# Far sums of a graph recurrence: four batches or eight in one matmul

## The chip, the cores and the metric

The kernel runs on one core of one Trainium2 chip. A time is the device time of one execution in microseconds. Before the change the median of three runs is 4688.69 us (4688.29 to 4690.42).

A core has engines with one instruction queue each, worked through in order: TensorE (matmuls, in the profile PE, with the weight loads as PEld), VectorE (DVE), ScalarE (ACT), GpSimd (POOL), and SyncE (SP), which only issues DMAs here. They wait for each other by semaphores. TensorE writes to PSUM[...].

## The reference, cut to what matters

Sixteen graphs (batches) of 1024 nodes with 256 features pass through four layers, each of the form x = x + layer(relu(layernorm(x)), adj). The change is in layer 2, a recurrence over the nodes:

```python
def step(h, i):
    x = jnp.take(h_e, i, axis=1)
    row = jnp.take(norm_adjT, i, axis=1)
    x_par = jnp.einsum('bj,bjd->bd', row, h)
    iou = x @ W_ioux.T + b_ioux + x_par @ W_iouh.T + b_iouh
    r, z = jnp.split(iou, 2, axis=1)
    r, z = (jax.nn.sigmoid(r), jax.nn.sigmoid(z))
    hc = jnp.tanh(x @ W_coux.T + b_coux + x_par * r @ W_couh.T + b_couh)
    h_new = z * x_par + (1.0 - z) * hc
    h = jax.lax.dynamic_update_slice(h, h_new[:, None, :], (0, i, 0))
    return (h, None)
h_out, _ = jax.lax.scan(step, h_e, jnp.arange(n))
```

Node i needs x_par, the weighted sum over all nodes j: the new h for j < i, the old one for j >= i. The matrix is sparse (some 3% of the entries), so nodes that do not depend on each other can be computed together.

## The kernel before, in words

Layers 0 and 1 run first, batch by batch, then the recurrence (layer 2), then layer 3. All arithmetic is in float32.

**The recurrence.** The 1024 nodes are cut into 8 blocks of 128 (index t in the code), and a block into 8 sub-blocks of S = 16 (index s, 0 to 7). A table made earlier orders the nodes within a block so that nodes in a sub-block mostly do not depend on each other. One step (t, s) computes the 16 nodes of a sub-block for all 16 batches, 256 columns in all: `x` is the sum over parents, `round_` (lines 817 to 849) makes the gates and the new state, first the r, z and c matmuls (line 788, tiles pr, pz, pc), then sigmoid and tanh on ScalarE (lines 829, 834, 835, 845) and the products on VectorE (lines 830, 839, 846, 847), ending in `hT`. `turned` (lines 851 to 860) transposes hT on TensorE (line 856) and copies it to `h` or `dh` on ScalarE (line 859). Sub-blocks 5 and 6 take a second round (line 995 on) for the dependencies inside a sub-block, with an exchange by `x_change` (line 813, copies `dx` in lines 988 and 989) between the rounds, and sub-block 7 takes four. A branch (line 1006) runs further rounds where a chain of dependencies is longer.

**What later sub-blocks get from a finished one.** With h of sub-block s in hand, its contributions are added: to the next sub-block at once (`near`, line 1029), to the next block's first sub-block in `next_block` (line 757), and to all that lie further ahead in the block in `far_tasks` (lines 761 to 780). The columns that the far sum of sub-block s covers are far = 128 - (s + 2) * 16 per batch: 96, 80, 64, 48, 32, 16 for s = 0 to 5, and none after. The batches come in two groups (G2 = 2) of eight (GB = 8). A far sum is one matmul of a 128-column slice of h with a masked, spread out adjacency `bd` (line 716, on GpSimd) into a PSUM tile `pf`, and one addition by VectorE of that tile to `bxt` (line 773), where the sums over parents are gathered.

**Fillers.** TensorE would wait for the other engines during a step. So each step has a list of tasks, `todo` (lines 919 to 938), mixed from two lists: `behind`, the far sums of the sub-block before, and `share`, the base products of the next block (`base_tasks`: seven matmuls of 256 columns at line 623 for each batch, a scaled copy `bs` to SBUF at line 610 with a 0/1 matrix `to` at line 607, and two transposes, the "turn", at line 637 with a copy at line 638). The far sums of sub-blocks 2 to 5 are therefore worked off in steps 3 to 6. A list is emptied in proportion, and steps of one round take base products while between 6 and 9 tasks are on the list (line 935).

`fill(weight)` (lines 942 to 948) pops tasks at a few places of the step until their summed costs, which each task carries as a number, reach that place's share. A task puts its matmuls into the program there, and its bank-emptying part on the list `late`, which `evict()` puts into VectorE's and ScalarE's program at the end of that stretch, behind the step's own arithmetic:

```python
late.append(task() or (lambda: None))
```

The order of TensorE, VectorE, ScalarE and GpSimd is that of the program text (line 884), so a change of a task's cost or length changes where all tasks stand.

**Banks.** Far sums, base products, turns and the gate matmuls (line 735) share the tile name pf with three buffers of one bank each. A matmul that needs a bank waits until the instruction that reads the earlier tile in it is done. A base product holds its bank over its seven matmuls and until its copy bs.

**DMA.** `load` (lines 588 to 597) fetches the adjacency `ab` and the states `hb` of a base product one batch ahead through SyncE's queue, and line 601 masks one 128x128 part on GpSimd. GpSimd also issues the gathers `aj` (line 700) and the scatters of h (line 1022).

Of the kernel before, what the change touches and what calls it, by code (L numbers as in the profile page):

```python
# [9 lines left out]
F32 = mybir.dt.float32  # L10
# [6 lines left out]
P = 128  # L17
B, N, D, H = 16, 1024, 256, 1024
NT = N // P
DC = D // P  # L20
HC = H // P
S = 16
NS = P // S
G2 = 2
GB = B // G2
# [15 lines left out]
def gnn_stack(ctx: ExitStack, tc: tile.TileContext, a: dict, out: bass.AP):  # L41
    nc = tc.nc
# [505 lines left out]
    def layer_2(shared, early):  # L548
        with ExitStack() as st:
            wp = st.enter_context(tc.tile_pool(name="w2", bufs=1))  # L550
            psum = st.enter_context(tc.tile_pool(name="psum2", bufs=1, space=PSUM))
# [201 lines left out]
            def next_block(h, bd, n, start):  # L753

                for c in range(DC):
                    for g in range(G2):
                        nc.tensor.matmul(pnx[:, c, g * GR : (g + 1) * GR], h[:, g, c * P : (c + 1) * P],
                                         bd[:, g, :, n : n + S], start=start and c == 0 and g == 0, stop=True,
                                         skip_group_check=True)

            def far_tasks(bxt, h, sub):


                bd, s = sub.bd, sub.s
                far = P - (s + 2) * S

                def task(g, c, b4):
                    def run():
                        pf = psum.tile([P, 4, far], F32, name="pf", bufs=3)
                        nc.tensor.matmul(pf, h[:, g, c * P : (c + 1) * P], bd[:, g, b4 : b4 + 4, S : S + far],  # L770
                                         start=True, stop=True)
                        to = bxt[:, c, g * GB + b4 : g * GB + b4 + 4, P - far :]
                        return lambda: nc.vector.tensor_add(to, to, pf)  # L773
                    return 0.0067 * far, run
                tasks = []
                if far > 0:
                    tasks = [task(g, c, b4) for g in range(G2) for c in range(DC) for b4 in (0, 4)]
                if sub.n > P - s * S:
                    tasks.insert(0, (0.9, lambda: next_block(h, bd, P - (s + 1) * S, s == 0)))
                return tasks  # L780
# [103 lines left out]
            with tc.manual_schedule(engines={mybir.EngineType.PE, mybir.EngineType.DVE, mybir.EngineType.Activation, mybir.EngineType.Pool}):  # L884
# [3 lines left out]
                bxt = shared.tile([P, DC, B, P], F32, name="bxt")  # L888
# [14 lines left out]
                for t in range(NT):  # L903
# [10 lines left out]
                    for s in range(NS):  # L914
# [38 lines left out]
                        for c in range(DC):  # L953
                            to = x[:, c].rearrange("p (b i) -> p b i", b=B)
# [13 lines left out]
                        h = work.tile([P, G2, D], F32, name="h")  # L968
# [56 lines left out]
                        if s + 1 < NS:  # L1025
                            near = psum.tile([P, DC, G2 * GR], F32, name="pa")
                            for c in range(DC):
                                for g in range(G2):
                                    nc.tensor.matmul(near[:, c, g * GR : (g + 1) * GR], h[:, g, c * P : (c + 1) * P],
                                                     sub.bd[:, g, :, :S], start=True, stop=True)  # L1030
                            behind = far_tasks(bxt, h, sub)
                        elif t + 1 < NT:
                            next_block(h, sub.bd, 0, False)
                            near = pnx
                            behind = last_tasks(t + 1, bxt_next)
                            bxt, he = bxt_next, he_next
# [302 lines left out]
    with tc.tile_pool(name="shared", bufs=2) as shared:  # L1339
        x, hn, at, h = {}, {}, {}, {}  # L1340
# [49 lines left out]
```

## Time and profile before

| what | value |
|---|---|
| median of three runs | 4688.69 us |
| profiled execution, its time | 4692.98 us |
| its span | 4691.1 us |
| granted TensorE clock, mean | 0.976 |
| recurrence, page time | 1522.6 to 3404.1 us |
| step 3 of block 1 | 1837.9 to 1862.9 us |
| step 4 of block 2 | 2105.7 to 2130.1 us |
| steps 5 and 6 of block 1 | 1895.2 to 1924.1, 1924.1 to 1952.8 us |
| matmuls of far sums (line 770) | 768 records, 214.5 us busy |
| additions of far sums (line 773) | 384, 141.5 us busy |
| base products (line 623) | 1568 records, 420.8 us busy |

A step is counted from one sum of x (line 956) to the next. In rows of the profile, an operation is given as output <- inputs, with partitions x columns; "xN" is a count; the bracket in a timeline row is the time that the engine stood idle ahead of it, and what ended that. A float32 matmul leaves two MATMUL records, and with them two weight loads. The recorded end of a matmul is modelled; how long one occupies TensorE is read from one start to the next.

The additions take, by columns (mean of 64 each): 0.552 us for 384, 0.486 for 320, 0.419 for 256, 0.352 for 192, 0.284 for 128 and 0.217 for 64.

### The profile page before, as it was taken

The page shows a single profiled execution, that of the slowest core. Times are in us where ns is not written, and L with a number is a line of the kernel's source. Part 1 is how long each engine was busy: PE and PEld are TensorE (multiplying, and loading weights), DVE is VectorE, ACT ScalarE, POOL GpSimd, SP SyncE. Part 2 cuts the span into 40 slices and gives each one's busy share as a digit, 9 for nine tenths or more (in the row PEclk, how much of TensorE's full clock was granted, in tenths as well). Part 3 has the DMA queues.
Part 4 walks back from the last instruction along what each step waited for, and adds up shares of the span by engine and source line. Part 5 has one row for each costly group of instructions (what it writes and reads, how often), then busy time and mean ns, then how long its engine had stood idle before and what let it go on. Part 6 is the DMA issues. An engine that isn't in the chain of part 4 may idle for free. (4 is left out here: it accounts for less than half of the span.)

```text
span 4691.1 us, 55474 instructions
## 1 busy us (share of the span) xinstructions
PE 4365.5 (93%) x19479; PEld 2999.7 (64%) x19479; DVE 2551.8 (54%) x6564; ACT 1280.5 (27%) x2741; POOL 1622.2 (35%) x1914
## 2 busy tenths in 40 slices
PE   8899799999897999999999999999899999999998
PEld 4444345555454777777778777777655656565666
DVE  6667945446544444444444444445456666666665
ACT  1111112221211232323232322222323333333332
POOL 3223234333432323232222233333245353535352
PEclk9999899999998999999999999999899999999999
DMA  4333234565545544444434444442042323232310
GB/s 148 120 110 96 87 92 162 180 204 163 163 136 186 158 127 148 130 153 137 149 110 155 132 144 146 158 132 84 31 157 81 108 81 108 81 108 81 108 45 19
DMA packets 530992, 576.81 MB, mean 123 GB/s; under 512 B 42544, under 2 KB 439472, under 8 KB 528304
## 3 DMA queue, kind: packets, MB, share of 16 engines
q1 hardware_dynamic: 499536, 460.27, 31.5%
q0 software_dynamic: 31040, 111.44, 6.7%
q8 instruction: 207, 3.39, 0.3%
q14 instruction: 209, 1.71, 0.1%
HBM read 469.65 MB, written 116.65 MB: 125 GB/s over the span
## 5 line engine op out<-in xcount | busy, mean ns | idle before, releaser
L295 PE MATMUL pa<-at,h 128*128 128x512 f32 x1088 | 495.3, 608 | 32.8 <-DVE ag L300 32.8
L623 PE MATMUL pf<-hb,ab 128*128 128x256 f32 x1568 | 420.8, 387 | 29.0 <-DVE bxt L773 16.3
L295 PE MATMUL pa<-at,q 128*128 128x512 f32 x960 | 424.7, 595 | 0.0
L295 PEld LDWEIGHTS pa<-at,h 128*128 128x128 f32 x1088 | 209.6, 195 | 277.3 <-issue 231.4
L735 PE MATMUL pf<-hs,wx 128*128 128x256 f32 x1536 | 348.8, 381 | 20.2 <-POOL hs L726 18.1
L735 PEld LDWEIGHTS pf<-hs,wx 128*128 128x128 f32 x1536 | 290.4, 191 | 62.8 <-POOL hs L726 19.9
L623 PEld LDWEIGHTS pf<-hb,ab 128*128 128x128 f32 x1568 | 278.7, 193 | 69.3 <-DVE bxt L773 23.5
L295 PEld LDWEIGHTS pa<-at,q 128*128 128x128 f32 x960 | 178.5, 190 | 216.6 <-issue 212.8
L1188 PE MATMUL ph<-bxt,hb 128*128 128x512 f32 x704 | 309.3, 595 | 3.9 <-ACT hb L1172 3.1
L1217 POOL TENSOR_TENSOR ss<-ss,sq 128x512 f32<-128x512 f32 x224 | 280.5, 1271 | 87.9 <-ACT sq L1215 84.1
L770 PE MATMUL pf<-bd,h 128*128 128x384 f32 (+5 forms) x768 | 214.5, 373 | 48.4 <-DVE bxt L773 26.5
L1022 POOL DMA_INDIRECT hs_d<-h,table x128 | 129.2, 1010 | 371.2 <-ACT gates L743 185.6
L1278 PEld LDWEIGHTS po<-w,hh 128*128 128x128 f32 x2048 | 236.2, 193 | 9.5 <-issue 7.2
L1278 PE MATMUL po<-w,hh 128*128 128x128 f32 x2048 | 240.3, 277 | 1.4 <-ACT hh L1261 0.7
L1188 PEld LDWEIGHTS ph<-bxt,hb 128*128 128x128 f32 x704 | 132.6, 191 | 163.9 <-issue 159.0
L773 DVE TENSOR_TENSOR bxt<-bxt,pf 128x384 f32<-128x384 f32 (+5 forms) x384 | 141.5, 385 | 146.8 <-PE pf L770 144.3
L740 DVE TENSOR_TENSOR gates<-pf,bias 128x512 f32<-128x512 f32 x128 | 88.3, 691 | 220.5 <-PE pf L735 220.5
L1260 DVE TENSOR_TENSOR hh<-hh,po 128x512 f32<-128x512 f32 x256 | 154.5, 681 | 96.7 <-PE po L1257 96.7
L83 POOL TENSOR_TENSOR rs<-rs_v,mhalf 128x8 f32<-128x8 f32 (+1 forms) x65 | 106.8, 1643 | 252.8 <-DVE rs_v L79 239.4
L770 PEld LDWEIGHTS pf<-bd,h 128*128 128x128 f32 x768 | 132.5, 192 | 93.2 <-DVE bxt L773 41.9
L1215 ACT ACTIVATE sq<-hh 128x512 f32<-128x512 f32 x224 | 141.2, 630 | 164.3 <-DVE hh L1213 126.2
L829 ACT ACTIVATE r<-pr 128x256 f32<-128x256 f32 (+3 forms) x230 | 68.0, 347 | 415.2 <-PE pr L788 400.9
(296 smaller groups left out, 8548.4 us busy)
## 6 DMA issues: line engine op xcount, KB each, us to landing
at<-in_adjT SPq DMA_DIRECT2D x64, 1024.0 KB, 7.0
ab<-in_adj SPq DMA_DIRECT2D x128, 512.0 KB, 3.8
bxt<-in_adjT SPq DMA_DIRECT2D x88, 512.0 KB, 6.4
at<-in_adjT SPq DMA_DIRECT2D x40, 512.0 KB, 6.6
ad<-in_adj SPq DMA_DIRECT2D x128, 128.0 KB, 6.7
x_d<-x POOLq DMA_DIRECT2D x16, 1024.0 KB, 5.4
he_d<-h POOLq DMA_DIRECT2D x16, 1024.0 KB, 8.9
heT_d<-hT POOLq DMA_DIRECT2D x16, 1024.0 KB, 4.4
```

Source lines behind the costliest of these rows:

```text
L83: nc.gpsimd.tensor_tensor(r, t, mhalf.to_broadcast(shape), ALU.pow)
L295: nc.tensor.matmul(pa, h[:, mt, c * P : (c + 1) * P], at[n0 // 512][:, mt], start=mt == 0, stop=mt == NT - 1)
L623: nc.tensor.matmul(pb, ab[:, jts[k]], hb[:, jts[k]], start=k == 0, stop=k == len(jts) - 1)
L735: nc.tensor.matmul(pg[:, e], wx[:, c, q * D + e * P : q * D + (e + 1) * P], self.hs[:, c], start=c == 0, stop=c == DC - 1)
L770: nc.tensor.matmul(pf, h[:, g, c * P : (c + 1) * P], bd[:, g, b4 : b4 + 4, S : S + far], start=True, stop=True)
L773: return lambda: nc.vector.tensor_add(to, to, pf)
L1022: nc.gpsimd.indirect_dma_start(out=hs_d[t][g][:, :], out_offset=row(1, g, t, s), in_=h[:, g], in_offset=None)
L1188: nc.tensor.matmul(pa, h[b][:, mt, c * P : (c + 1) * P], at[b][n0 // NH][:, mt], start=mt == 0, stop=mt == NT - 1)
L1215: nc.scalar.activation(sq, hh[q][:, k], AF.Square)
L1217: nc.gpsimd.tensor_tensor(ss[q], ss[q], sq, ALU.add)
L1260: nc.vector.tensor_mul(hh[q][:, k], hh[q][:, k], pr)
L1278: nc.tensor.matmul(po[:, n], left[:, c, n * P : (n + 1) * P], right[:, c], start=onto is None and n == 0 and c == 0, stop=c == HH - 1, ski ...
```

## The change

Where eight batches fit into one bank (far * 8 <= 512, so for sub-blocks 2 to 5), a far sum takes all eight batches of a group: matmuls of 512, 384, 256 and 128 columns take the place of two each of 256, 192, 128 and 64, and one addition that of two. Sub-blocks 0 and 1 (768 and 640 columns for eight) stay as they are. The cost that a task carries changes with it, from 0.0067 * far for four batches to 0.0017 * far for each batch (0.0136 * far for eight).

```diff
                 far = P - (s + 2) * S
-
-                def task(g, c, b4):
+                n = 4 if far * GB > 512 else GB
+
+                def task(g, c, b0):
                     def run():
-                        pf = psum.tile([P, 4, far], F32, name="pf", bufs=3)
-                        nc.tensor.matmul(pf, h[:, g, c * P : (c + 1) * P], bd[:, g, b4 : b4 + 4, S : S + far],
+                        pf = psum.tile([P, n, far], F32, name="pf", bufs=3)
+                        nc.tensor.matmul(pf, h[:, g, c * P : (c + 1) * P], bd[:, g, b0 : b0 + n, S : S + far],
                                          start=True, stop=True)
-                        to = bxt[:, c, g * GB + b4 : g * GB + b4 + 4, P - far :]
+                        to = bxt[:, c, g * GB + b0 : g * GB + b0 + n, P - far :]
                         return lambda: nc.vector.tensor_add(to, to, pf)
-                    return 0.0067 * far, run
+                    return 0.0017 * n * far, run
                 tasks = []
                 if far > 0:
-                    tasks = [task(g, c, b4) for g in range(G2) for c in range(DC) for b4 in (0, 4)]
+                    tasks = [task(g, c, b0) for g in range(G2) for c in range(DC) for b0 in range(0, GB, n)]
```

One line more stands in the function, so lines from 767 on carry a number higher by one in the changed kernel.

## The prediction

> **What bounds the kernel now.** I read the shares of busy time first, then the costliest groups, the waits of TensorE inside the recurrence, and the timeline of single steps. "Step s" is sub-block s (0 to 7) of a block; the far sums of sub-blocks 2 to 5 run as fillers in steps 3 to 6, so these steps change. In the page, TensorE has 93% of the span, and the two groups that the change touches are these.
>
> ```profile
> PE 4365.5 (93%) x19479; PEld 2999.7 (64%) x19479; DVE 2551.8 (54%) x6564; ACT 1280.5 (27%) x2741; POOL 1622.2 (35%) x1914
> ...
> L770 PE MATMUL pf<-bd,h 128*128 128x384 f32 (+5 forms) x768 | 214.5, 373 | 48.4 <-DVE bxt L773 26.5
> ...
> L773 DVE TENSOR_TENSOR bxt<-bxt,pf 128x384 f32<-128x384 f32 (+5 forms) x384 | 141.5, 385 | 146.8 <-PE pf L770 144.3
> ```
>
> A float32 matmul leaves two records, so 768 are 384 far sums, 64 of each of six widths. TensorE idles ahead of them for the adds that empty their banks. The waits of the weight loads (PEld), which run ahead of the matmuls, within the recurrence (page time 1547 to 3430 us; in total, times, longest):
>
> ```profile
> PEld pf L770 <- DVE bxt L773: 41.9, 39, 2.0
> PEld pf L623 <- DVE bxt L773: 23.5, 18, 1.4
> PEld pf L770 <- ACT bs L610: 21.3, 21, 1.1
> PEld pf L770 <- DVE bxt L638: 14.7, 14, 1.1
> ```
>
> All four are one thing, a wait for one of the three "pf" banks: 101.4 us together. Is it on the path? In the timeline of block 1, step 3 (start, duration):
>
> ```profile
> 1846.58 1.03 PE L623 MATMUL pf<-hb,ab 128*128 128x256 f32 x4
> 1847.44 1.03 PE L770 MATMUL pf<-bd,h 128*128 128x256 f32 x4
> ...
> 1848.54 0.49 ACT L610 ACTIVATE bs<-pf,dinv 128x256 f32<-128x256 f32 x1
> 1849.08 0.70 PE L770 MATMUL pf<-bd,h 128*128 128x256 f32 x2 [0.61 <-ACT bs L610]
> ...
> 1849.68 0.42 DVE L847 TENSOR_TENSOR hT<-z,w 128x256 f32<-128x256 f32 x1
> ...
> 1850.22 1.08 DVE L773 TENSOR_TENSOR bxt<-bxt,pf 128x256 f32<-128x256 f32 x3
> 1850.69 0.70 PE L623 MATMUL pf<-hb,ab 128*128 128x256 f32 x2 [0.91 <-DVE bxt L773]
> ...
> 1853.73 0.60 PE L856 MATMUL pa<-ident,hT 128*128 128x128 f32 x4
> ```
>
> hT is done at 1850.10, but the transposes that need it (L856) start at 1853.73: they are queued on TensorE behind fillers, and the fillers stand still twice for a bank, whose add sits on VectorE behind the very chain that makes hT. So bank waits lengthen the step one for one. Step 5 has the larger case:
>
> ```profile
> 1903.85 0.42 DVE L847 TENSOR_TENSOR hT<-z,w 128x256 f32<-128x256 f32 x1
> 1904.20 0.28 DVE L773 TENSOR_TENSOR bxt<-bxt,pf 128x128 f32<-128x128 f32 x1
> ...
> 1904.53 0.49 PE L770 MATMUL pf<-bd,h 128*128 128x128 f32 x2 [1.57 <-DVE bxt L773]
> ...
> 1905.94 0.60 PE L856 MATMUL pa<-ident,hT 128*128 128x128 f32 x4
> ```
>
> **What the skill says.** "VectorE: DVE Perf Modes", section on the TRN2 errata, gives a float32 tensor_tensor (N+151)/0.96 ns: 691 at 512 columns, 424 at 256. The trace has 692 (L740) and 419, so one add of 512 for two of 256 saves 0.146 us; it agrees. "PSUM — Partial Sum Buffer", the four PSUM rules: one matmul output is at most one bank, 512 fp32; eight batches of 64 columns are just that. "Perfetto Trace Analysis", Identifying Performance Opportunities: a gap that repeats on the engine that should be saturated can mean too few buffers; that is what the four rows show. "TensorE: Matmul & The Clock Gate", Part 1: after an idle window of about 3.4 us TensorE runs at half rate; in block 7, steps 5 and 6, this trace has 128-column passes 0.21 us apart where elsewhere they are 0.11.
>
> **The change, part by part.** 128 matmuls and 128 adds go (4 steps x 8 blocks x 4). From starts in the timelines one far sum takes 0.43 us on TensorE at 256 columns, 0.86 at 512, 0.33 at 192, 0.65 at 384, 0.22 at 128, and 0.17 to 0.22 at 64. Pairs are free of gain except the narrowest: 4 x 8 x about 0.17 = 5 us. VectorE loses 128 x 0.14 = 18 us of work, which lies beside TensorE's and is worth nothing by itself. The gain is in banks: a merged sum holds one where two held two. The built order of TensorE, in steps of blocks 0 to 6, between the last candidate matmul ("pc") and the transposes T:
>
> Before, steps 3 and 4: 2 base, 3 far, base, far, base, turn, far, 2 base, T. After: 3 base, far, 2 base, far, turn, 2 base, T. Before, step 5: far, turn, base, far, 2 base, far, T; after: turn, base, far, 2 base, T.
>
> *Step 3* (base product 0.43, turn 0.22). Before: 4.95 us of work in 7.15, so 2.2 of stall. After: base end 1847.88, far 1848.74, 2 base 1849.60. The second far takes the bank of the finished base product; its "bs" copies come 0.43 later than before, since that product ends 0.43 later (free at 1849.46): no wait, end 1850.46. The turn needs the first far's bank. Its add follows hT, which is itself 0.43 late because the tanh stands behind the "bs" copy on ScalarE: start 1850.65, 0.69 long, so turn at 1851.39, T at 1852.47. Gain 1.26.
>
> *Step 4* (block 2, from its start): pc ends 8.47 (a smaller first filling, 0.11), base 9.77, far 10.42, 2 base 11.28, second far from 11.41 ("bs" ends 11.36) to 12.06, first add 12.54 to 13.10, turn 13.15, T 14.23 against 15.38. Gain 1.15.
>
> *Step 5* (block 1, from its start). pc ends 6.74. Turn, base, far and 2 base need three banks and wait for none: they end at 8.68 and T waits for hT instead. Block 7 shows that state: in its step 5 T ends 2.69 after pc, and the exchange (L813) starts 0.96 later, behind the copies of "dh". So T ends 9.43, base and far fit in, L813 at 10.39 (before 12.15). Then 0.87 of exchange and 1.73 of fillers: the second round begins at about 13.03 (14.43). It keeps its 3.47, so pc ends at 16.50; turn, 2 base, far, base 1.94: T at 18.44 (20.76). After it two base instead of two base and a far: 0.22. Gain 2.54.
>
> *Step 6*, likewise: L813 at 10.39 (12.00), round 12.80 (14.20), pc end 16.23, T ends 18.40 (21.02), 0.22 after. Gain 2.84.
>
> Per block 7.79, times seven 54.5. Block 7 has no base products: in step 3 T ends at 8.55 instead of 10.00, and one 512-column sum follows it instead of a 256 one (0.43): 1.0; step 4 by the same count 0.6, steps 5 and 6, where T waits for hT already, 0.2 and 0.1: 2.0. Sum 56.5.
>
> Moves with no price: in steps 3 and 4 the mask of a base block (L601, 0.30) goes on GpSimd from ahead of the two gathers "aj" (L700, about 1 us each) to behind them, some 2 us later. Its consumer is half a step away, and what is queued behind it waits for r at 6.8 anyway; if that cover were gone, 2 us a step. In steps 5 and 6 "dx" (L989) passes a "bs" copy on ScalarE, which can only help. The DMA queue's order is unchanged; base blocks land 8 us or more before use in these steps, so shorter steps don't run into them. After T each step is TensorE work (12 gate matmuls, 5.2 us), so nothing else catches up.
>
> The profiled execution took 4692.98 (span 4691.1), the median run is 4.3 less: 4692.98 - 56.5 = 4636.5, as a median 4632.2.
>
> **Rivals.** (a) The wait only moves: the longer add (0.69) that frees the first far's bank stops the turn in steps 3 and 4 for all that was gained, and only 5 and 6 gain: 7 x 5.4 + 0.3 = 38, so 4651. If instead steps 5 and 6 find their end in another chain (GpSimd's "bd", "dh" copies), 7 x 2.4 + 1.6 = 18: 4670. For: VectorE empties banks only after hT. Against: the order leaves banks free. (b) Hidden: T would have waited for hT anyway, and only narrow matmuls gain, 5 us: 4684. Against: T starts 3.6 us after hT in step 3. (c) Slower: the waits for hT in steps 5 and 6 put TensorE into half rate, as in block 7. One window of 3.41 us costs up to 1.7; from 56.5 / 1.7 = 33 windows it eats the gain, two in each of the 28 steps (95) give 4727. For: block 7 shows it without base products. Against: the new waits are 0.5 us, and steps with 2 us of stall ran at full rate (the 1.00 in these rows is the granted clock; ahead of it stand the stretch, its length and the busy us of TensorE, its weight loads, VectorE, ScalarE and GpSimd):
>
> ```profile
> 1837.90:1862.90 25.00, 23.38 (x118) 19.73 (x117) 10.96 (x25) 6.26 (x16) 8.36 (x15) 1.00 0.43 126
> ...
> 1895.20:1924.10 28.90, 26.33 (x154) 22.67 (x153) 12.17 (x37) 8.45 (x23) 9.05 (x16) 1.00 0.37 115
> ```
>
> **How the numbers follow.** Main case 0.78, partial gains (a) 0.13, hidden (b) 0.05, slower (c) 0.04. Within the main case I allow 15 us each way for waits not counted: new ones of half a microsecond in each of the 28 steps, or half-rate windows lost (two stand in step 4 of blocks 3 and 5, some 1.6 us each). So 4632; the range reaches down to 4616 and up past the first case of (a), to 4655. A difference of 0.2% (9 us) is about what a measurement can tell: faster 0.92, same 0.04, slower 0.04.
>
> **What would show it.** Steps 3 to 6 of about 23.8, 23.2, 26.4 and 25.9 us (25.0, 24.4, 28.9, 28.7 now), other steps as they were; the four rows of bank waits fall from 101 to about 45, and waits of L856 for hT rise. There are 128 merged sums in place of 256 in these steps. I am wrong if T in step 5 doesn't start at about 8.7, or if step 3 still stands for two banks.

## The result and the profile after

| | before | after |
|---|---|---|
| median time | 4689.28 us | 4623.35 us |
| lowest and highest of four runs | 4688.29, 4690.42 | 4619.34, 4624.45 |
| profiled execution, its time | 4692.98 us | 4624.45 us |
| its span | 4691.1 us | 4622.5 us |

The ratio of the times is 0.9864, with a 95% interval from 0.9852 to 0.9875, which is 58.6 to 69.4 us less. The prediction was 4632.0 (4616 to 4655): the time lies in the range, 8.7 us under the predicted value.

The first lines are from the page of the kernel after, the shares of busy time and the two groups concerned. Its lines are one number on: the far sum is L771, its addition L774, the transposes T are L857 and the exchange is L814.

```profile
PE 4336.9 (94%) x19223; PEld 2956.2 (64%) x19223; DVE 2535.5 (55%) x6436; ACT 1279.5 (28%) x2741; POOL 1623.5 (35%) x1914
...
L771 PE MATMUL pf<-bd,h 128*128 128x384 f32 (+4 forms) x512 | 185.6, 454 | 5.3 <-ACT bs L610 2.8
...
L774 DVE TENSOR_TENSOR bxt<-bxt,pf 128x384 f32<-128x384 f32 (+4 forms) x256 | 125.0, 501 | 97.0 <-PE pf L771 95.5
```

The records of the far matmul fell from 768 to 512 (two records are one matmul), the additions from 384 to 256. VectorE has 16 us less to do, and TensorE's idle time ahead of the far sums fell from 48.4 us to 5.3 (part of it now stands ahead of the turn, as the next rows show).

The waits of the weight loads inside the recurrence (page time 1530 to 3350 us; total, times, longest):

```profile
PEld pf L637 <- DVE bxt L774: 22.2, 20, 1.6
PEld pa L857 <- DVE hT L848: 18.8, 39, 0.6
PEld pf L771 <- DVE bxt L774: 10.9, 23, 1.5
PEld pf L771 <- ACT bs L610: 10.1, 21, 0.9
PEld pf L623 <- DVE bxt L774: 8.2, 6, 1.4
```

With the 3.6 us that the turn (L637) waits for the copy `bs`, these waits for a bank are 55.0 us. Before, the four rows that the prediction shows were 101.4 us, and the turn's two small rows, for `bs` and for additions, another 3.6 and 1.3 over the whole recurrence. The transposes wait for hT for 18.8 us instead of 11.3: in some steps the chain that makes the new state is now what they wait for, not the bank.

Step 3 of block 1, the one shown of before, now starts at 1826.94 us (timeline: start, duration, engine, and in brackets the idle time and what ended it; "..." stands for rows left out):

```profile
1835.62 1.46 PE L623 MATMUL pf<-hb,ab 128*128 128x256 f32 x6
...
1836.92 1.02 PE L771 MATMUL pf<-bd,h 128*128 128x512 f32 x2
...
1837.78 1.03 PE L623 MATMUL pf<-hb,ab 128*128 128x256 f32 x4
...
1838.64 1.04 PE L771 MATMUL pf<-bd,h 128*128 128x512 f32 x2
...
1839.16 0.42 DVE L848 TENSOR_TENSOR hT<-z,w 128x256 f32<-128x256 f32 x1
...
1839.69 1.28 DVE L774 TENSOR_TENSOR bxt<-bxt,pf 128x512 f32<-128x512 f32 x2
...
1840.43 0.44 PE L637 MATMUL pf<-to,bs 128*128 128x128 f32 x2 [0.75 <-DVE bxt L774]
...
1840.71 1.03 PE L623 MATMUL pf<-hb,ab 128*128 128x256 f32 x4
...
1841.58 0.60 PE L857 MATMUL pa<-ident,hT 128*128 128x128 f32 x4
```

The second far sum follows the two base products without a wait. Of the two stalls one is left, ahead of the turn (L637), and it has the cause that the prediction gave it: its bank is emptied by an addition that stands on VectorE behind hT. From the second far sum to the turn TensorE has 0.86 us of work in 1.79, so the stall is 0.9 us; the 0.75 in the bracket counts from the modelled end of the matmul. T starts 14.63 us after the start of the step; before, it was 15.84 (1853.73 less the start at 1837.89).

Step 5 of the same block starts at 1881.92:

```profile
1889.31 0.59 PE L771 MATMUL pf<-bd,h 128*128 128x256 f32 x2
...
1889.74 1.03 PE L623 MATMUL pf<-hb,ab 128*128 128x256 f32 x4
...
1890.59 0.42 DVE L848 TENSOR_TENSOR hT<-z,w 128x256 f32<-128x256 f32 x1
1890.60 0.90 PE L857 MATMUL pa<-ident,hT 128*128 128x128 f32 x4
...
1891.07 0.20 PEld L857 LDWEIGHTS pa<-ident,hT 128*128 128x128 f32 x2 [0.32 <-DVE hT L848]
...
1892.30 0.41 PE L814 MATMUL pa<-ai,dh 128*128 128x64 f32 x2
```

No filler waits for a bank here. T takes up the first half of hT as soon as the fillers end, at 8.68, and it takes 0.90 us instead of 0.60 since its third weight load waits 0.32 us for the second half. The exchange starts 10.38 us into the step, where it was 12.15.

The steps as stretches (length; busy us of TensorE, its weight loads, VectorE, ScalarE, GpSimd; granted clock; share and rate of the DMAs): step 3 of block 1, step 4 of block 2, steps 5 and 6 of block 1.

```profile
1826.90:1850.80 23.90, 23.05 (x111) 18.30 (x110) 10.08 (x22) 6.37 (x16) 8.51 (x15) 1.00 0.46 146
2080.50:2103.80 23.30, 22.37 (x111) 18.26 (x110) 9.73 (x21) 6.33 (x16) 8.06 (x15) 1.00 0.48 139
1881.90:1908.20 26.30, 25.95 (x146) 22.44 (x146) 11.63 (x32) 8.30 (x23) 8.91 (x16) 1.00 0.41 126
1908.20:1934.20 26.00, 25.23 (x146) 21.91 (x146) 11.10 (x32) 8.43 (x24) 7.18 (x15) 1.00 0.73 207
```

Step 5 was 28.90 long with 26.33 us of TensorE work; now it is 26.30 with 25.95. It has lost its idle time, hardly any of its work. No other engine is near full in these stretches.

Read off the two traces by the starts of the steps (the page's stretches, rounded to 0.1, agree), the time went thus:

| where | change of the span, us |
|---|---|
| steps 3, 4, 5, 6 of all eight blocks | -9.5, -12.7, -18.1, -20.0: together -60.4 |
| other steps of the recurrence | -9.9 (of it step 0: -8.9) |
| outside the recurrence | about +1.7 |

The first row holds the steps that the change edits: 52.6 us are the same four gains repeated in blocks 0 to 6, 3.2 are block 7, and 4.5 are three executions of step 4 (blocks 0, 3 and 5) that were 1.3 to 1.6 us longer than the others before and are not now. The second row has no edit in it. It and the smaller parts of the first come back below.

### The profile page after: what moved, and what is told of

Its sections match the earlier page's. It is cut to its first block, busy times and chain, and to the rows that moved or that the text cites. A ratio compares the mean times of both kernels' runs of the same rounds, so it can differ in the third digit from the quotient of the medians.

```text
span 4622.5 us, 54868 instructions
## 1 busy us (share of the span) xinstructions
PE 4336.9 (94%) x19223; PEld 2956.2 (64%) x19223; DVE 2535.5 (55%) x6436; ACT 1279.5 (28%) x2741; POOL 1623.5 (35%) x1914
## 5 line engine op out<-in xcount | busy, mean ns | idle before, releaser
L623 PE MATMUL pf<-hb,ab 128*128 128x256 f32 x1568 | 407.9, 383 | 14.5 <-DMA hb<-hs_d 5.7
L771 PE MATMUL pf<-bd,h 128*128 128x384 f32 (+4 forms) x512 | 185.6, 454 | 5.3 <-ACT bs L610 2.8
L1214 DVE SCALAR_TENSOR_TENSOR hh<-ph,b,u 128x512 f32<-128x512 f32 x192 | 144.0, 751 | 64.9 <-PE ph L1210 54.8
L774 DVE TENSOR_TENSOR bxt<-bxt,pf 128x384 f32<-128x384 f32 (+4 forms) x256 | 125.0, 501 | 97.0 <-PE pf L771 95.5
```

Of the source, the lines that this page charges most:

```text
L623: nc.tensor.matmul(pb, ab[:, jts[k]], hb[:, jts[k]], start=k == 0, stop=k == len(jts) - 1)
L1214: nc.vector.scalar_tensor_tensor(hh[q][:, k], ph, b1[:, k : k + 1], u, op0=ALU.add, op1=ALU.add)
```

## The experiments

Five questions: do the gains of the wide sums (steps 3 and 4) and of the narrow ones (steps 5 and 6) arise separately; is it the banks, the order or the costs; is it the longer matmul; is it VectorE's saved work; and does the stall that is left in step 3 have the cause given. The diffs are against the kernel after. The first four were timed beside the kernel before at 4687.81 us (23 runs), the others beside it at 4685.83 (6 runs).

**Only the wide sums merged** (64 and 48 columns a batch, worked off in steps 3 and 4).

```diff
-                n = 4 if far * GB > 512 else GB
+                n = GB if far in (64, 48) else 4
```

> Only the far sums of sub-blocks 2 and 3 (512 and 384 columns) are merged, so steps 3 and 4 change and 5 and 6 stay as before. Bank theory (a merged sum holds one bank where two held two, and the transposes stop waiting behind stalled fillers): steps 3 and 4 shorten by 1.2 and 1.1 us in each of seven blocks and by 1.5 together in the last: 18 us, about 4671. Rival, that some common cause outside these steps (step 0, half-rate windows) gives most of the gain: 4640 or less, or no gain. Steps 5 and 6 should read 28.9 and 28.7 us.

Measured: 4657.58 us (4655.90 to 4660.98), ratio 0.9922 (0.9899 to 0.9945). Steps 3 and 4 of its trace are 23.83 and 23.27 us long, as after; steps 5 and 6 are 28.8 to 28.9 and 28.63, as before. Over the eight blocks, steps 3 and 4 change by -9.3 and -12.9 us and steps 5 and 6 by about nothing. The time is 13 us below what was expected. By the trace some 4.5 of it are the three long executions of step 4, and the rest is in steps that this kernel shares with the one before: -10.7 us.

**Only the narrow sums merged** (32 and 16 columns, steps 5 and 6).

```diff
-                n = 4 if far * GB > 512 else GB
+                n = GB if far in (32, 16) else 4
```

> Only the far sums of sub-blocks 4 and 5 (256 and 128 columns) are merged. Bank theory: steps 5 and 6 shorten by 2.55 and 2.65 us in seven blocks, and by some 1 us in the last: 37 us, about 4652; steps 3 and 4 read 25.0 and 24.4 us. If the two halves do not add up to the whole gain of 66 us, the rest (about 10 us) belongs to neither and is in steps that the change does not touch.

Measured: 4645.71 us (4633.48 to 4650.94), ratio 0.9889 (0.9863 to 0.9915). Steps 5 and 6 are 26.31 and 26.00 as after (-16.7 and -20.1 us over the blocks), steps 3 and 4 are 25.05 and 24.38 as before. The time is 6 us below what was expected. The two halves do their work in their own steps and nowhere else. Their gains in time, 30 and 42 us, make 72, more than the 64 to 66 of the whole. In each of the two traces, as in that of the kernel after, steps 0, 1, 2 and 7, which no edit touches, are together 8 to 11 us shorter than in the first trace of before; a gain that comes once with either half is counted twice in the sum.

**The order and the costs of after, but two matmuls in two banks and two additions.**

```diff
-                        pf = psum.tile([P, n, far], F32, name="pf", bufs=3)
-                        nc.tensor.matmul(pf, h[:, g, c * P : (c + 1) * P], bd[:, g, b0 : b0 + n, S : S + far],
-                                         start=True, stop=True)
-                        to = bxt[:, c, g * GB + b0 : g * GB + b0 + n, P - far :]
-                        return lambda: nc.vector.tensor_add(to, to, pf)
+                        out = []
+                        for k in range(b0, b0 + n, 4):
+                            pf = psum.tile([P, 4, far], F32, name="pf", bufs=3)
+                            nc.tensor.matmul(pf, h[:, g, c * P : (c + 1) * P], bd[:, g, k : k + 4, S : S + far],
+                                             start=True, stop=True)
+                            out.append((bxt[:, c, g * GB + k : g * GB + k + 4, P - far :], pf))
+                        return lambda: [nc.vector.tensor_add(to, to, pf) for to, pf in out]
```

> The costs, the task list and so the order of the changed kernel, but each task makes two matmuls of four batches into two banks with two additions, as before the change. Bank theory: the gain goes: transposes at about 15.4 in step 3 (15.8 before, 14.6 after), at about 10.6 in step 5 (10.8 before, 9.2 after), in all about 7 us below the kernel before, 4682, within 6 either way. Order theory (the gain comes from where the costs put the tasks): 4625 to 4630 as after.

Measured: 4685.03 us (4673.66 to 4700.85, 20 runs), ratio 0.9993 (0.9983 to 1.0002). The gain is gone, though tasks stand where they stand after. In step 3 of block 1, T starts 15.70 us into the step (15.84 before, 14.63 after). The timeline of its step 5 of block 1, which starts at 1890.28 (here the far matmul is L773, the turn's copy L638, T is L859):

```profile
1897.67 0.39 PE L773 MATMUL pf<-bd,h 128*128 128x128 f32 x2
...
1898.95 0.42 DVE L850 TENSOR_TENSOR hT<-z,w 128x256 f32<-128x256 f32 x1
1899.29 0.42 DVE L638 COPY bxt<-pf 128x256 f32<-128x256 f32 x1
...
1899.76 0.49 PE L773 MATMUL pf<-bd,h 128*128 128x128 f32 x2 [1.71 <-DVE bxt L638]
...
1900.09 1.03 PE L623 MATMUL pf<-hb,ab 128*128 128x256 f32 x4
...
1900.95 0.60 PE L859 MATMUL pa<-ident,hT 128*128 128x128 f32 x4
```

The second half of the pair finds no bank: the turn's is emptied by a copy that VectorE reaches only after hT. TensorE stands 1.71 us, and T starts 10.67 us into the step, where it is 8.68 after. The step is 28.93 long, as before. Two rows of its waits:

```profile
PEld pf L773 <- DVE bxt L638: 40.7, 38, 1.9
PEld pf L773 <- DVE bxt L776: 26.1, 39, 1.8
```

So the gain is not the new order of tasks, nor their mixing by other costs.

**One bank and one addition, but two matmuls of four batches into it.**

```diff
-                        nc.tensor.matmul(pf, h[:, g, c * P : (c + 1) * P], bd[:, g, b0 : b0 + n, S : S + far],
-                                         start=True, stop=True)
+                        for k in range(0, n, 4):
+                            nc.tensor.matmul(pf[:, k : k + 4], h[:, g, c * P : (c + 1) * P],
+                                             bd[:, g, b0 + k : b0 + k + 4, S : S + far], start=True, stop=True)
```

> One bank and one addition for eight batches, as after, but two matmuls of four batches each into that bank. Bank theory: the gain stays, less up to 5 us for the narrowest matmuls (64 columns): 4623 to 4629. Theory that longer matmuls are what pays: 4680 or more.

Measured: 4625.92 us (4623.73 to 4636.87), ratio 0.9861 (0.9834 to 0.9887). Steps 3, 4 and 5 are as after in most blocks. Step 6 of block 1, as a stretch with the columns as above, is the exception:

```profile
1906.00:1932.40 26.40, 26.01 (x154) 22.84 (x154) 11.22 (x32) 8.28 (x23) 7.00 (x14) 1.00 0.73 207
```

It has eight more matmul records (154 for 146) and is 0.44 us longer by the starts of the steps (26.44 for 26.00); over seven blocks that is 3 us. No more than that is the wider matmul's by the steps.

**One matmul and one bank, but two additions of four batches.**

```diff
-                        to = bxt[:, c, g * GB + b0 : g * GB + b0 + n, P - far :]
-                        return lambda: nc.vector.tensor_add(to, to, pf)
+                        def out():
+                            for k in range(0, n, 4):
+                                to = bxt[:, c, g * GB + b0 + k : g * GB + b0 + k + 4, P - far :]
+                                nc.vector.tensor_add(to, to, pf[:, k : k + 4])
+                        return out
```

> As after, one matmul and one bank for eight batches, but two additions of four batches. Bank theory: the turn in steps 3 and 4 waits 0.1 us longer, no more: 1 to 3 us over after, 4624 to 4627. Theory that the saved VectorE time (18 us) is what pays: 4640.

Measured: 4626.34 us (4625.12 to 4630.21), ratio 0.9876 (0.9859 to 0.9894). Steps 3 and 4 are 0.12 us longer each (23.96 and 23.40), since there the turn waits for the end of an emptying, and the pair of additions ends later than the single one. Steps 5 and 6 are as after. VectorE's saved additions are therefore worth 1.7 us at the most by the steps (0.24 x 7).

These two kernels can't be told in time from the one after, nor the one with two banks from the one before. What pays is the number of banks that a far sum holds. (Two matmuls and two additions at once in one bank were not run; that their sum does nothing more is taken from the two single runs and from the 1.71 us wait for a bank above.)

**The kernel before, traced once more.** No edit; it serves for how much of a difference in untouched steps two traces of one kernel show.

> The kernel before once more, for a second trace of it. If step 0 (229 us over the eight blocks in the first trace, 218 to 221 in three of the changed kernels) gives part of the gain, it reads 227 or more again; if it was chance of one execution, 218 to 224. Half-rate windows in step 4, two in the first trace, should be there again in one to three blocks.

Measured: one execution of 4690.88 us, span 4688.8. Step 0 sums to 225.0 us over the blocks, against 229.3 in the first trace and 220.4 after. This lies between the two cases of the expectation. So 4 us of step 0's 8.9 lie within what two traces of the same kernel differ by. By the clock records, step 4 of blocks 0, 1 and 2 holds a window of half rate, so three blocks, as expected. Stretches (columns as above): step 4 of block 2, step 3 of block 1, and within the first the 10 us from 2110.

```profile
2101.10:2127.10 26.00, 24.13 (x118) 20.82 (x117) 10.29 (x26) 6.31 (x16) 7.88 (x14) 0.93 0.42 129
1833.20:1858.30 25.10, 23.48 (x119) 19.83 (x118) 10.97 (x26) 6.35 (x16) 8.46 (x15) 1.00 0.46 128
2110.00:2120.00 10.00, 8.23 (x36) 6.85 (x35) 4.09 (x12) 2.04 (x6) 0.78 (x3) 0.83 0.47 144
```

This step 4 took 26.00 us with a granted clock of 0.93, where the same step without a dip takes 24.38. The timeline inside it:

```profile
2112.17 0.59 PE L770 MATMUL pf<-bd,h 128*128 128x192 f32 x2 [0.82 <-ACT bs L610]
...
2113.71 1.08 PE L623 MATMUL pf<-hb,ab 128*128 128x256 f32 x2 [0.94 <-DVE bxt L773]
...
2114.57 0.85 PE L770 MATMUL pf<-bd,h 128*128 128x192 f32 x2
```

From the start of the base product's matmul to that of the next one is 0.86 us; at full rate the same is 0.43. The clock records put the start of the window 0.2 us after this matmul's, so right behind the two bank stalls.

**The copy `bs` and the matrix `to` made once.** In all kernels so far a base product that is turned at once makes its copy and its matrix a second time: `summed` decides by `state`, which the turn has already emptied by then; four base products a block do. Line 610 so runs 140 times where 112 are needed. In step 3 of block 1 of the kernel after, the first copy, which the turn needs, stands ahead of the tanh (L846). The second copy stands behind it, and the second `to` (L607) stands on VectorE between hT and the additions, whose first one frees the bank that step 3 still waits for:

```profile
1837.12 0.47 ACT L610 ACTIVATE bs<-pf,dinv 128x256 f32<-128x256 f32 x1 [1.94 <-PE pf L623]
...
1837.49 0.65 ACT L846 ACTIVATE hc<-pc 128x256 f32<-128x256 f32 x2
...
1838.02 0.49 ACT L610 ACTIVATE bs<-pf,dinv 128x256 f32<-128x256 f32 x1
...
1839.50 0.28 DVE L607 TENSOR_SCALAR to<-step,place 128x128 f32<-128x128 f32 x1
1839.69 1.28 DVE L774 TENSOR_TENSOR bxt<-bxt,pf 128x512 f32<-128x512 f32 x2
```

```diff
-                loaded, state = {}, {}
+                loaded, state, done = {}, {}, set()
...
-                    if b not in state:
+                    if b not in done:
+                        done.add(b)
```

> As after, but the scaled copy bs and its matrix to, which four base products of each block make twice, are made once. VectorE then starts the first far addition of steps 3 and 4 some 0.2 us earlier, and the turn with it: 14 steps, 3 us, with step 2 perhaps 5: 4618 to 4621. If the ScalarE copy were what the stall hangs on, 10 us.

Measured: 4618.10 us (4610.38 to 4623.53), ratio 0.9853 (0.9835 to 0.9872), in time not to be told from the kernel after. By the steps, 2, 3 and 4 are 0.20 us shorter each: the additions start 0.19 us after the second `to` in the rows above, and that is what goes. The first copy still stands ahead of the tanh. In the kernel before, too, the first stall of step 3 (0.61 us, in the prediction's rows) ends with a second copy, the one at 1848.54; how much of the gain that kernel would have kept without its second copies was not run.

**And the turn three tasks later**, so that the copy that it needs is no longer put ahead of the tanh.

```diff
-                        tasks[-1].insert(2, last)
+                        tasks[-1].insert(5, last)
```

> As one_copy, and the turn of a base product stands three tasks later in the list, so that its scaled copy no longer stands ahead of the tanh on ScalarE in steps 3 and 4, and hT and the additions behind it come 1.5 us sooner. If the last stall of 0.9 us in steps 3 and 4 is the wait of the turn for the first far sum's bank, it goes: T at about 13.7 instead of 14.6, 7 x 2 x 0.9 = 13 us, about 4610. If T is then held by something else, as after.

Measured, with the edit of the kernel ahead of it: 4611.37 us (4608.99 to 4614.76), ratio 0.9844 (0.9827 to 0.9862). Its step 3 of block 1 starts at 1825.75 (tanh is L847, the copy `bs` L611, hT L849, T L858):

```profile
1834.90 0.66 ACT L847 ACTIVATE hc<-pc 128x256 f32<-128x256 f32 x2 [0.70 <-PE pc L790]
...
1835.92 0.47 ACT L611 ACTIVATE bs<-pf,dinv 128x256 f32<-128x256 f32 x1 [0.37 <-PE pf L624]
...
1836.57 0.43 DVE L849 TENSOR_TENSOR hT<-z,w 128x256 f32<-128x256 f32 x1
...
1837.44 0.68 DVE L775 TENSOR_TENSOR bxt<-bxt,pf 128x512 f32<-128x512 f32 x1
1837.45 1.07 PE L772 MATMUL pf<-bd,h 128*128 128x512 f32 x2
...
1838.35 1.46 PE L624 MATMUL pf<-hb,ab 128*128 128x256 f32 x6
...
1839.64 0.60 PE L858 MATMUL pa<-ident,hT 128*128 128x128 f32 x4
```

The copy stands behind the tanh, hT is done at 11.25 us instead of 12.64, and none of these matmuls waits for a bank any more. T starts 13.89 us into the step instead of 14.63, and the steps 2, 3 and 4 shrink to 24.97, 22.92 and 22.25; step 1 pays 0.69 (22.29). This is below the kernel before by 74 us (4685.83 beside it) and below the one after by 9 to 12, by the ratios and by the medians; the intervals of the two ratios still overlap a little. It agrees with the prediction's reading of the rest, that the 0.9 us ahead of the turn in step 3 came from an addition behind an hT that was itself behind a copy. But the edit also takes the turn itself out of the place where it waited, and the two effects were not separated.

## Why the prediction was right

**The mechanism.** Its claim was that the gain is in banks, not in TensorE's or VectorE's work. Two banks in the same order gave 0.9993; one bank with two matmuls gave 0.9861, one bank with two additions 0.9876, and the change itself 0.9864. The claim stands. Rival (b), that only narrow matmuls gain, falls with the kernel that merges only the wide sums: its steps 3 and 4 gain 9.3 and 12.9 us. The pointer was two facts read together: in step 3 hT is done 3.6 us ahead of the transposes that need it, and TensorE stands still in between for banks. In one reading the prediction's words go too far: it has both stalls wait for an addition behind hT. The second does; the first (0.61 us) waits, as its own row says, for a copy `bs` on ScalarE, behind the tanh. The replay of the step does count these copies.

**The step lengths.** Every one of the four is within 0.2 us.

| step | gain predicted | measured in blocks 0 to 6 | T's start (steps 3, 4) or end (5, 6) from the step's start, predicted | measured |
|---|---|---|---|---|
| 3 | 1.26 | 1.21 | 14.58 | 14.63 |
| 4 | 1.15 | 1.10 | 14.23 | 14.28 |
| 5 | 2.54 | 2.56 | first T 9.43, last 18.44 | 9.43, 18.40 |
| 6 | 2.84 | 2.64 | last T 18.40 | 18.52 |

(A step starts with its first addition to x, line 957 after. T ends where the next matmul starts.) The exchange of step 5 was put at 10.39 and came at 10.38. The lengths came out because every one was made by replaying the built order of TensorE with the durations of the trace and asking of each matmul which of three banks it takes and what empties it. Step 6 lost 0.12 of its 0.2 us in the second round, which began at 12.91 and not 12.80. Block 7 gained 3.2 us and not 2.0 (the four terms given for it, 1.0, 0.6, 0.2 and 0.1, make 1.9). Of this 1.44 is in step 6, where 0.1 was counted, and it is not shown to be the change's: in the ten traces this step takes 24.1 to 24.2 us with one half-rate window of 3.41 us and 25.3 to 25.7 us with twice that, and the kernel with two banks, which gains nothing, has 24.12. The sum over these steps, without the three long executions of step 4, is 52.6 + 3.2 = 55.8; the prediction had 56.5. That the two are so close is in part luck.

**The rivals.** Rival (a) had its grain: the longer addition does stop the turn in step 3, for 0.75 us. But this was in the sum, and the wait that took the place of the two old ones is the smaller. Rival (c), that the new short waits for hT would bring half rate, went the other way: there was less of it after the change.

**What was mis-sized.** The measured gain of the medians is 65.9 us, 9.4 more than the sum of 56.5. The term that was too small is the one for half-rate windows, which the prediction saw in step 4 of blocks 3 and 5 ("some 1.6 us each") and put into the range and not into the sum. These two gave back 3.2 us. The third long execution of step 4 (block 0, 1.3 us) holds no such window; there TensorE stood 1.0 us near the start of the step, for a reason that no view names. The other part, -8 to -11 us in steps that no edit touches, was in no term ("other steps as they were"); most of it is step 0, and the last section shows that it goes with half-rate windows too. The bank waits were put at 45 and came out at 55, of which 22.2 are the turn's. That cost nothing, since the moments of T held.

Of the sizes on which little rested: 5 us for narrower matmuls measured 3. One addition of 512 for two of 256 was to save 0.146 us of VectorE's time and saves 0.154 (0.684 for 2 x 0.419), and in time that saving was worth nothing in steps 5 and 6, as said.

## What to carry to other kernels

Where a filler's result is emptied by an engine that also carries the critical chain, as here, count banks, not only work: replay the order of the matmuls against the moments at which banks come free, and price a change by the moment at which the critical matmul then starts. Two halves of one result that are emptied together are better put into one bank when banks are short, even where neither the matmul nor the emptying gets cheaper by it. And after a stall is gone, look at what the next one waits for: here a matrix made a second time for nothing, ahead of the addition that frees the bank, and the place of one task were worth another 9 to 12 us together.

## What was not expected of the hardware

A step with two stalls of about 1 us, TensorE otherwise busy, can lose its full rate. In three executions with the old form of step 4 (two of the kernel before, one of the kernel with only the narrow sums merged), 8 of 24 step-4 executions hold a window of half rate by the clock records of the trace (3.41 us long), and each is longer by some 1.6 us: 25.99 for 24.38 in the usual case. (Two of them, in block 0, take 26.79 and 26.91; their fillers came to the first stall 0.8 and 0.9 us later than in the other blocks.) In six executions with merged sums in step 4, there is none in 48. The kernel with two banks has none in step 4 either, but in step 6 of blocks 2, 4 and 5, whose length then is 30.5 us and not 29.0 (32.25 in block 5, where it lasts twice as long). "TensorE: Matmul & The Clock Gate" of the Trainium skill, in the section on the second failure mode (cycling through PSUM banks), says that short idle times between groups of matmuls can make the clock swing between half and full rate. These runs agree for step 4. They don't say what decides: the old step 3 has stalls of like size (0.61 and 0.91 us) and shows no window in its 24 executions in the same three traces.

Over the whole recurrence the time at half rate is 78.5 us and 68.3 us in the two traces of before, 68.3 with two banks and with only the narrow sums merged, 54.6 with only the wide ones, and 44.4 to 47.8 after and in all four kernels built on it. At half rate at most half of the time is lost, so by estimate up to 12 to 17 us of the gain can lie there, which would cover the 9.4.

The same records, taken for step 0 alone, say where. Step 0 sums to 229.3 and 225.0 us over the blocks in the two traces of before, with 28.3 and 19.1 us at half rate, and to 216 to 221 in the other eight traces, with 7.7 to 15.6. From the first trace of before to the one after, its half-rate time fell by 18.1 us and its length by 8.9; from the second, by 8.9 and 4.7. Both lengths are about half of the half-rate time that went, so the half rate can account for all of it; no run turns it on or off by itself to show that it does. The kernel with two banks fits: its step 0 has 10.2 us at half rate and sums to 221.4, and its whole is as high as in the second trace of before because of step 6 (17.1 us, where both traces of before have 6.8). Why step 0 keeps its full rate for longer when other steps are edited, no run shows.
